# Placing the loads in a slot's DMA queue, and one of two masked copies of q on ScalarE

## The chip, the cores and the metric

The kernel runs on one core of a Trainium2 chip. The metric is the time on the device in microseconds, taken from the slowest core, which here is the only one; lower is better. Before the change three runs gave 944.01 us as their median (943.09 to 948.07).

The engines are named as in the profile: PE multiplies matrices, DVE (VectorE) and POOL (GpSimd) do elementwise work, ACT (ScalarE) applies functions and copies, SP (SyncE) issues nearly all transfers. Each engine works through its own list of instructions in order, and waits at an instruction whose inputs or buffers are not ready.

## The reference

Sixteen sequences of 256 tokens with 256 features go through one cross-attention layer and then one decoder block. All of it is float32, with 16 heads of 16 features.

```
layer 0   q = rmsnorm(x) Wq;  k, v = rmsnorm(ctx) Wk, Wv
          x = rmsnorm(x + attention(q, k, v) Wo)
layer 1   h = layernorm(x);  q, k, v from h, q and k rotated (rope)
          x = x + causal attention(q, k, v) Wo + bias
layer 2   h = layernorm(x);  q from h, k and v from ctx, q and k rotated
          x = x + attention(q, k, v) Wo + bias
MLP       x = x + gelu(layernorm(x) W1 + b1) W2 + b2
```

With 16 sequences there are 48 attentions, and 16 MLPs that are done two sequences at a time.

## The kernel before

**Slots.** The main loop `for i in range(N_ATT)` (L983) has 48 passes, which this text calls slots; slot i does the scores and exponentials of attention i. `ORDER` says which layer each is of: the three layers are interleaved, so that the sequences move through them at different times. The layers of slots 4 to 8 are 1 only in 5 and 7; causal slots followed by one of layer 1 or 2 are slots 21, 28, 38, 40 and 42, and each of those five is followed by layer 2. Batches are loaded for the layer-0 attentions, `xT` and `yT` (turned, 256 KB each), `cur` and `y` (by token, 256 KB each).

**Blocks of a slot.** A slot has four blocks, or three when the attention is causal. Block n writes the scores S of one piece (`scores`, L551), followed on PE by the products of the piece before with v (`values`, L590). ACT turns S into exponentials pt (L562), on causal ones POOL then zeroes what lies above the diagonal (L569). Between blocks PE gets one dense product each: the next attention's q in block 0, its k in block 1, its v in the block before the last, and an older attention's output projection in the last. A causal slot has k and v both in block 1.

**q and k.** A head has 16 features, but a row group of PE has 32 partitions. So two heads share a group and q is kept twice in tile `qm`, once with the odd heads set to zero and once with the even ones: for layers 1 and 2, `q` (L474) multiplies the rotated q by two `parity` columns, on DVE (L487). Rotating (`rotated`) takes ACT's two bias activations (L461), then on DVE a shuffle (L465), two products (L469) and a sum, L485 for q and L510 for k (`kT`). The scores of slot i+1 need both halves of its qm and its kT. For layer 0, nothing is rotated: `q` writes both halves on DVE (L480), and ACT copies kT (L512).

**The way of the sums.** The products with v also give each row's sum of exponentials, as one more column. For an attention, ACT copies the first half of the result out of PSUM (`take`), DVE the second one slot later (`end`, L607), and both halves go to DRAM (`hop`, L608). From there the sums are read back alone (L615), then the rest (`oT`, L620). `invert` takes their reciprocal on DVE (L627), sends it to DRAM (`inv_hop`, L629) and reads it back spread over partitions (`inv`, L635). A slot later `divide` (L641) multiplies. In non-causal slots k follows `invert` in DVE's list, in causal ones it comes ahead of it.

**The SP queue.** Transfers are issued by SP in program order, and SP stands still at one whose input isn't ready. In a slot the order is: the second `hop` of attention i-1, its `sums` and `oT`, the four `hT` of a normalized input that was sent through DRAM (L450) if there is one, then loads (first call of `load_next`, L1015), `inv_hop`, `inv`, `rq` for layer 0, loads again (second call, L1043), the first `hop` of attention i, and `turn_hop` (L441) if an input is sent out. `load_next` (L976) takes its loads from the list `due`: eleven pieces of weights, and ahead of them the four of a batch whose layer-0 attention is three slots ahead. It takes two at a call in a slot with such a batch, otherwise one (none in the first slots).

**Statistics.** A layer-0 attention's `stats` read `cur` and `y` on DVE (L254) two slots before its own.

After the slots follow the MLPs, from about 717 us on.

Of the kernel before, what the change touches and what calls it, by code (L numbers as in the profile page):

```python
# [11 lines left out]
AF = mybir.ActivationFunctionType  # L12
ALU = mybir.AluOpType
# [15 lines left out]
N_ATT = 3 * B  # L29
# [44 lines left out]
def xattn_kernel(  # L74
# [21 lines left out]
    nc = tc.nc  # L96
# [23 lines left out]
    def batch(b):  # L120

        xTs[b] = work.tile([P, KC, S], F32, tag="xT", name=f"xT{b}", bufs=3)
        yTs[b] = work.tile([P, KC, S], F32, tag="yT", name=f"yT{b}", bufs=Y_LIVE)
        ys[b] = work.tile([P, NC, D], F32, tag="y", name=f"y{b}", bufs=3)
        return [
            (rows_of(b), x[b].rearrange("(c p) d -> p c d", p=P)),
            (ys[b], y[b].rearrange("(c p) d -> p c d", p=P)),
            (xTs[b], xt[b].rearrange("(k p) s -> p k s", p=P)),
            (yTs[b], yt[b].rearrange("(k p) s -> p k s", p=P)),
        ]  # L130
# [218 lines left out]
    class Att:  # L349
# [121 lines left out]
                )  # L471
            return a, u

        def q(self):  # L474
            ps = by_feature(self.hT, self.w, 0)
            self.qm = work.tile([P, KC, 2, S], F32, tag="qm", name="qm", bufs=2)
            if self.layer == 0:
                rq = self.rq.unsqueeze(1).to_broadcast([P, KC, S])
                for i in range(2):
                    nc.vector.scalar_tensor_tensor(  # L480
                        self.qm[:, :, i, :], ps, parity[i], rq, ALU.mult, ALU.mult
                    )
                return
            a, u = self.rotated(ps, 0)
            nc.vector.tensor_tensor(a, a, u, ALU.add)  # L485
            for i in range(2):
                nc.vector.tensor_scalar(self.qm[:, :, i, :], a, parity[i], None, ALU.mult)  # L487

        def first_qk(self):

# [171 lines left out]
    def att(i):  # L662
        if i is not None and 0 <= i < N_ATT:
            return atts.setdefault(i, Att(i))
        return None

    def do(i, *names):
        a = att(i)
        for name in names:
            if a is not None:  # L670
                getattr(a, name)()
# [266 lines left out]
    with tc.manual_schedule():  # L938
# [34 lines left out]
            due.append((fc2_sb[:, 2 * j : 2 * j + 2], fc2[j * D : (j + 1) * D]))  # L973
        due = [(t, w.rearrange("(k p) n -> p k n", p=P)) for t, w in due]

        def load_next(i):  # L976
            n = 2 if i > 1 and ahead is not None and ahead.layer == 0 else int(i > 2)
            for t, w in due[:n]:
                nc.sync.dma_start(out=t, in_=w)
            del due[:n]  # L980

        turns = turned_ahead()
        for i in range(N_ATT):  # L983
            a, last = att(i), att(i - 1)
            sent, due_turn = turns.get(i), i + 2 if i + 2 not in turns.values() else None
            fresh = sent is not None and att(sent).below == i - 3
            ahead = att(i + 3)
            if i > 1 and ahead is not None and ahead.layer == 0:
                due[:0] = batch(ahead.b)

            finishing = i >= 3 and att(i - 3).layer == 0
            follows = finishing and i + 2 < N_ATT and att(i + 2).below == i - 3
            for n in range(len(a.blocks)):
                if n == 0 and a.causal and not finishing:
                    do(due_turn, "stats")
                a.scores(n)
                if n > 0:
                    a.values(n - 1)  # L1000
                elif last is not None:
                    last.values(-1)
                final = len(a.blocks) - 1
                if n == 0:
                    if i == 0:
                        a.v()
                        do(1, "spread")
                    late = finishing and i + 2 < N_ATT and att(i + 2).layer == 0
                    if not follows and not late and (finishing or not a.causal):
                        do(due_turn, "stats")  # L1010
                    if sent is not None and not fresh:
                        do(sent, "stats")
                    do(i - 1, "end")
                    do(turns.get(i - 1), "pieces_in")
                    load_next(i)  # L1015
                    if late:
                        do(due_turn, "stats")
                    do(i - 3, "finish")
                    if follows:
                        do(due_turn, "stats")  # L1020
                    if fresh:
                        do(sent, "stats")
                    if not finishing:
                        do(due_turn, "norm")
                    if i == N_ATT - 3:
                        mlps[0].stats()
                    if i == N_ATT - 2:
                        mlps[0].norm()
                    do(i - 2, "divide")
                    if i == N_ATT - 1:  # L1030
                        mlps[0].turn(nc.vector.tensor_copy)
                        mlps[0].keep()
                    do(i + 1, "q")
                elif n == 1:

                    if a.causal:
                        do(i + 1, "k")
                    if last is not None:
                        last.invert(lambda: do(i + 2, "send"))
                    else:  # L1040
                        do(i + 2, "send")
                    do(i + 2, "receive")
                    load_next(i)  # L1043
                    if not a.causal:
                        do(i + 1, "k")
                    if finishing:
                        do(due_turn, "norm")
                    for j in kept.get(i, ()):
                        att(j).keep()
                    if i == N_ATT - 1:  # L1050
                        do(i - 2, "project")
                        mlps[1].norm()
                if n == final - 1:
                    do(i + 1, "v")
                    do(sent, "pieces_out")
                    if i == N_ATT - 2:
                        mlps[1].stats()
                    if i == N_ATT - 1:
                        mlps[0].up(2)
                        mlps[0].mix("hT", HT_LIVE)  # L1060
                if n == final:
                    if i == N_ATT - 1:
                        mlps[1].turn(nc.vector.tensor_copy)
                    else:
                        do(i - 2, "project")
                    do(due_turn, "turn")
                if i == 0 and n == 0:
                    load(4)
                    nc.sync.dma_start(out=bias_sb, in_=rows.partition_broadcast(P))
                    nc.sync.dma_start(out=turn_sb, in_=turn)  # L1070
                if i == 0 and n == 1:
                    load_w(ca_sb, ca[:1], nc.sync)
                if i == 1 and n == 0:
                    load_w(sao_sb, [sa_o], nc.sync)
                if i == 1 and n == 2:
                    nc.sync.dma_start(
                        out=rope_sb, in_=rope.rearrange("(c p) t d -> p c t d", p=P)
                    )
                if i == 1 and n == 3:
                    att_hop = fold_bias(  # L1080
                        [(sa_sb, j * D, V_B1) for j in range(3)] + [(ca_sb, 0, V_B2)]
                    )
                if i == 2 and n == 2:
                    att_cols = fold_back(att_hop)
                    row_v = fc2_sb[:, 0]
                    nc.sync.dma_start(out=row_v, in_=att_hop[2].partition_broadcast(P))
                if i == 2 and n == 3:
                    fold_gain(sa_sb, slice(0, 3 * D), V_G1)
                if i == 3 and n == 3:
                    fold_att(att_cols, row_v)  # L1090
                if i == 8 and n == 2:
                    fold_gain(ca_sb, slice(0, D), V_G2)
                if i == 11 and n == 3:
                    fc1_hop = fold_bias([(fc1_sb, j * D, V_B3) for j in range(4)])
                if i == 12 and n == 1:
                    fc1_cols = fold_back(fc1_hop)
                if i == 14 and n == 2:
                    fold_fc1(fc1_cols)
                if i in (14, 15) and n == 1:
                    fold_gain(fc1_sb, slice(0, FF), V_G3, [i - 14], nc.gpsimd)  # L1100
                if n == 1 and i > 15 and not a.causal:
                    next(combined, None)
# [488 lines left out]
```

## Time and profile before

| | |
|---|---|
| median of three runs (lowest to highest) | 944.01 us (943.09 to 948.07) |
| the profiled execution: its time, its span | 935.7 us, 933.8 us |
| granted PE clock | 0.999 |
| busy PE / DVE / ACT / POOL | 920.2 / 679.2 / 533.2 / 314.0 us |
| second mask and first mask of q, DVE L487 | 64 instructions, 34.1 us |
| DVE idle until sums had landed, L626 and L627 | 15.4 and 13.1 us, 7 and 8 times |
| DVE idle until inv had landed, L641 | 13.0 us, 8 times |
| DVE idle until cur or y had landed, L254 | 1.7 us, 3 times, and 0.2 us, once |
| SP until hop had landed, L615; until inv_hop had landed, L635 | 120.0 us and 76.2 us |
| moved by the DMA engines | 95.26 MB, 102 GB/s over the span |

The span runs from the first to the last instruction of one profiled execution. A group of the profile gives line, engine, operation, output and input, how often, busy time and mean duration in ns, and then the idle time ahead of it with what ended it. In the timeline each line has its start, its duration, engine, source line and operation; "x2" means two instructions in one row. The duration of a DMA row is that of its issue on SP, not of the transfer. Busy time on an engine with idle time costs nothing by itself; what counts is which wait ends last ahead of the engine that sets the time.

### The profile page before, as it was taken

Reading aid. Unit: us, or ns where it says so; the run is one execution under the profiler, and the core shown is the slowest. Engines: PE = TensorE matmul, PEld = TensorE weight load, DVE = VectorE, ACT = ScalarE, POOL = GpSimd, SP = SyncE. Lnnn points to the kernel's source line nnn. Section 1 sums busy time; section 2 is a strip of 40 time slices with the busy share of each in tenths; the row PEclk is TensorE's granted clock in tenths of the full one; section 3 lists DMA queues with packets and bytes.
Section 4 is the critical chain, followed back from the end, with each engine's and each line's share of the span. In section 5 each row is a group of like instructions: output and inputs, shape, how many; then the busy total and the mean of one; then the engine's idle time right before and its main releaser. Section 6 shows DMA issues by size and latency. Waiting matters only on the chain.

```text
span 933.8 us, 29304 instructions
## 1 busy us (share of the span) xinstructions
PE 920.2 (99%) x12266; PEld 540.2 (58%) x12266; DVE 679.2 (73%) x1486; ACT 533.2 (57%) x749; POOL 314.0 (34%) x503
## 2 busy tenths in 40 slices
PE   8999999999999999999999999999999999999997
PEld 4444444445454544454454445455444799999997
DVE  4458677886878787868966878897887566667663
ACT  4666655766666665756656666666666634344440
POOL 4213543324444464443533434344033121122200
PEclk9999999999999999999999999999999999999999
DMA  9434454454334343432435433223222100000001
GB/s 297 155 100 126 128 170 136 132 159 125 124 106 144 94 129 98 152 111 84 141 121 157 132 106 98 90 86 102 92 76 82 36 24 23 20 4 24 24 24 48
DMA packets 115550, 95.26 MB, mean 102 GB/s; under 512 B 23498, under 2 KB 112210, under 8 KB 115410
## 3 DMA queue, kind: packets, MB, share of 16 engines
q1 hardware_dynamic: 114722, 92.77, 31.8%
q8 instruction: 98, 1.61, 0.7%
q10 hardware_dynamic: 688, 0.54, 0.2%
q14 instruction: 42, 0.34, 0.1%
HBM read 57.08 MB, written 36.20 MB: 100 GB/s over the span
## 4 chain that ended last, share of the span: by engine, by line
PE 78%; DVE 11%; DMA 5%; issue 2%; SPq 2%; POOL 2%; ACT 1%; DVEq 0%
PE S L551 15%; PE A L590 14%; PE d L341 13%; PE d L329 13%; PE upX L752 6%; PE A L850 5%; PE downZ L850 3%; PE upZ L752 3%; DVE u L469 2%; PE d L850 2%; DVE a L469 2%; PE d L752 2%; DVE u L465 1%; PE d L286 1%; DMA hop<-av 1%
## 5 line engine op out<-in xcount | busy, mean ns | idle before, releaser
L562 ACT ACTIVATE pt<-S 128x1024 f32<-128x1024 f32 x224 | 217.3, 1022 | 135.3 <-PE S L551 135.0
L551 PE MATMUL S<-qm,kT 32*128 32x512 f32 (+1 forms) x1536 | 202.8, 599 | 4.1 <-DVE kT L510 3.6
L590 PE MATMUL A<-pt,va 128*32 128x256 f32 (+1 forms) x3072 | 191.2, 367 | 1.3 <-POOL pt L569 0.7
L590 PEld LDWEIGHTS A<-pt,va 128*32 128x32 f32 x3072 | 80.5, 109 | 157.0 <-issue 92.7
L562 ACT ACTIVATE pt<-S,sy 128x1024 f32<-128x1024 f32 x128 | 135.7, 1111 | 50.8 <-PE S L551 50.5
L569 POOL TENSOR_SCALAR_AFFINE_SELECT pt<-pt 128x512 f32<-128x512 f32 x128 | 90.7, 725 | 147.5 <-ACT pt L562 146.6
L551 PEld LDWEIGHTS S<-qm,kT 32*128 32x128 f32 x1536 | 62.8, 183 | 76.0 <-issue 41.2
L317 POOL TENSOR_TENSOR cur<-cur,bias 128x512 f32<-128x512 f32 x48 | 68.7, 1438 | 56.5 <-DVE xn L271 56.5
L461 ACT ACTIVATE a<-d,qk_bias 128x256 f32<-128x256 f32 x128 | 53.8, 471 | 52.5 <-PE d L329 31.1
L329 PE MATMUL d<-hT,sa 128*32 128x256 f32 x1024 | 61.1, 379 | 0.0
L246 POOL TENSOR_SCALAR r_ln<-bmv 128x2 f32<-128x2 f32 x48 | 15.3, 318 | 118.0 <-DVE bmv L265 116.5
L469 DVE TENSOR_TENSOR u<-u,turn 128x512 f32<-128x512 f32 x64 | 52.2, 816 | 0.0
L469 DVE TENSOR_TENSOR a<-a,turn 128x512 f32<-128x512 f32 x64 | 49.8, 777 | 2.2
L641 DVE TENSOR_TENSOR oT<-oT,inv 128x512 f32<-128x512 f32 x48 | 39.2, 818 | 14.2 <-DMA inv<-inv_hop 13.0
L607 DVE COPY av<-A 128x512 f32<-128x512 f32 x47 | 32.2, 684 | 22.7 <-PE A L590 22.3
L465 DVE STREAM_SHUFFLE u<-a 128x512 f32<-128x512 f32 x64 | 47.4, 741 | 0.0
L790 ACT ACTIVATE g<-g,fb 128x256 f32<-128x256 f32 x96 | 41.0, 499 | 11.1 <-DVE g L779 11.1
L329 PEld LDWEIGHTS d<-hT,sa 128*32 128x32 f32 x1024 | 33.2, 110 | 22.0 <-issue 0.2
L246 POOL TENSOR_SCALAR r_o<-ms_o 128x2 f32<-128x2 f32 x16 | 3.9, 242 | 122.3 <-DVE sq L254 112.7
L650 DVE TENSOR_TENSOR cur<-d,cur 128x512 f32<-128x512 f32 x32 | 21.6, 676 | 29.0 <-PE d L341 29.0
L271 DVE TENSOR_SCALAR xn<-cur,bmv,r_ln 128x256 f32<-128x256 f32 x96 | 41.5, 481 | 0.8 <-POOL r_ln L247 0.8
L845 DVE TENSOR_TENSOR g<-g,g 128x512 f32<-128x512 f32 x64 | 40.9, 681 | 0.0
(148 smaller groups left out, 1556.0 us busy)
## 6 DMA issues: line engine op xcount, KB each, us to landing
hop<-av SPq DMA_DIRECT2D x96, 256.0 KB
oT<-hop SPq DMA_DIRECT2D x96, 128.0 KB
inv<-inv_hop SPq DMA_DIRECT2D x96, 128.0 KB
turn_hop<-turn SPq DMA_DIRECT2D x23, 256.0 KB
hT<-turn_hop SPq DMA_DIRECT2D x92, 64.0 KB
xT<-in_xt SPq DMA_DIRECT2D x16, 256.0 KB
cur<-in_x SPq DMA_DIRECT2D x16, 256.0 KB
yT<-in_yt SPq DMA_DIRECT2D x16, 256.0 KB
```

What stands on the lines that cost most here:

```text
L317: nc.gpsimd.tensor_tensor(t, t, bias_sb[:, row : row + D].unsqueeze(1).to_broadcast([P, NC, D]), ALU.add)
L329: nc.tensor.matmul(o, lhsT=w[:, k, at + t * P + j : at + t * P + j + 32], rhs=tokens, start=(k == 0), stop=(k == KC - 1), skip_group_check ...
L341: nc.tensor.matmul(ps[j : j + 32, c * D : (c + 1) * D], lhsT=some_tokens(src, k, c, j), rhs=w[:, k, at : at + D], start=(k == 0), stop=(k ...
L461: nc.scalar.activation(a[:, t], ps[:, t], AF.Identity, bias=bias[:, t : t + 1])
L465: nc.vector.stream_shuffle(u.rearrange("p t s -> p (t s)"), a.rearrange("p t s -> p (t s)"), SWAP)
L469: nc.vector.tensor_tensor(t, t, table.unsqueeze(1).to_broadcast([P, KC, S]), ALU.mult)
L551: nc.tensor.matmul(ps[:, j, 2 * m * u : 2 * m * (u + 1)] .rearrange("p (i s) -> p i s", i=2), lhsT=self.kT[r, t, kc * P : (kc + 1) * P], r ...
L562: nc.scalar.activation(pt[:, :, :w], ps[:, :, :w], AF.Exp, scale=scale)
L569: nc.gpsimd.affine_select(out=diag, in_=diag, compare_op=ALU.is_ge, fill=0.0, base=0, pattern=[[0, 2], [0, 2], [1, P]], channel_multiplier=-1,
L590: nc.tensor.matmul(self.av[32 * r : 32 * r + 32, i, q0:S], lhsT=self.va[:, kc, 8 * t + 2 * r + i, :], rhs=pts[r // 2][:, r % 2, i * m : (i ...
L752: nc.tensor.matmul(banks[c // 2][:, (c % 2) * S : (c % 2 + 1) * S], lhsT=a[:, c * P : (c + 1) * P], rhs=b, start=(first and c % 2 == 0), s ...
L850: nc.tensor.matmul(ps[:, c, :], lhsT=a[f // 2][:, f % 2, c * P : (c + 1) * P], rhs=b[:, f, :], start=(first and c == 0 and f == 0), stop=True,
```

## The change

It has two parts.

The loads are called at three places of a slot in place of two. A batch's `cur` and `y` go ahead of the slot's first work, so ahead of the second `hop` of the attention before; `xT` stays behind `inv` and `rq`; `yT` moves from there to the end of the slot, behind the first `hop` and `turn_hop`. Of the weights one is taken at the start of a slot and one behind `inv`, none at the end; in a slot with a batch up to two at the start, one behind `inv` and one at the end are taken from the list, the batch first.

In a causal slot whose next attention is of layer 1 or 2 (the five named above) DVE writes only the first half of qm. The second half is written by ACT from the same rotated q, as a copy with the parity column as its scale. It stands in ACT's list behind k's two bias activations, ahead of the exponentials of the last block. The order of PE's and of POOL's instructions is unchanged.

```diff
-        def q(self):
+        def q(self, both=True):
...
             nc.vector.tensor_tensor(a, a, u, ALU.add)
-            for i in range(2):
-                nc.vector.tensor_scalar(self.qm[:, :, i, :], a, parity[i], None, ALU.mult)
+            nc.vector.tensor_scalar(self.qm[:, :, 0, :], a, parity[0], None, ALU.mult)
+            self.rotated_q = a
+            if both:
+                nc.vector.tensor_scalar(self.qm[:, :, 1, :], a, parity[1], None, ALU.mult)
+
+        def second_mask(self):
+            if self.layer > 0:
+                nc.scalar.activation(
+                    self.qm[:, :, 1, :], self.rotated_q, AF.Copy, scale=parity[1]
+                )
...
-        def load_next(i):
-            n = 2 if i > 1 and ahead is not None and ahead.layer == 0 else int(i > 2)
+        def load_next(i, n, later):
+
+            if not (i > 1 and ahead is not None and ahead.layer == 0):
+                n = later if i > 2 else 0
             for t, w in due[:n]:
                 nc.sync.dma_start(out=t, in_=w)
             del due[:n]
...
             if i > 1 and ahead is not None and ahead.layer == 0:
                 due[:0] = batch(ahead.b)
+            load_next(i, 2, 1)
...
                     do(turns.get(i - 1), "pieces_in")
-                    load_next(i)
...
-                    do(i + 1, "q")
+                    if i + 1 < N_ATT:
+                        att(i + 1).q(both=not a.causal)
                 elif n == 1:
                     if a.causal:
-                        do(i + 1, "k")
+                        do(i + 1, "k", "second_mask")
...
                     do(i + 2, "receive")
-                    load_next(i)
+                    load_next(i, 1, 1)
...
                     do(due_turn, "turn")
+                    load_next(i, 1, 0)
```

## The prediction

> **What bounds the kernel now.** I read the page's busy times first, then its groups, then who PE waited for, and last the timeline around those waits.
>
> ```profile
> span 933.8 us, 29304 instructions
> ...
> PE 920.2 (99%) x12266; PEld 540.2 (58%) x12266; DVE 679.2 (73%) x1486; ACT 533.2 (57%) x749; POOL 314.0 (34%) x503
> ...
> L551 PE MATMUL S<-qm,kT 32*128 32x512 f32 (+1 forms) x1536 | 202.8, 599 | 4.1 <-DVE kT L510 3.6
> ```
>
> PE is busy 920.2 of 933.8 us at a granted clock of 0.999, and the change adds or removes no matmul. So at most the 13.6 us of PE's idle time can be won. The largest named part of it is 3.6 us of scores waiting for kT; the rest lies at the start, in hundredths between matmuls, or in the MLP tail, which the change does not touch. The timeline of PE shows the eight waits singly (the last bracket is the idle time and its releaser):
>
> ```profile
> 119.16 1.14 PE L551 MATMUL S<-qm,kT 32*128 32x512 f32 x8 [0.94 <-DVE kT L510]
> 339.69 1.14 PE L551 MATMUL S<-qm,kT 32*128 32x512 f32 x8 [0.37 <-DVE kT L510]
> 355.98 1.14 PE L551 MATMUL S<-qm,kT 32*128 32x512 f32 x8 [0.59 <-DVE kT L510]
> 442.04 1.14 PE L551 MATMUL S<-qm,kT 32*128 32x512 f32 x8 [0.37 <-DVE kT L510]
> 587.55 1.14 PE L551 MATMUL S<-qm,kT 32*128 32x512 f32 x8 [0.36 <-DVE kT L510]
> 616.31 1.14 PE L551 MATMUL S<-qm,kT 32*128 32x512 f32 x8 [0.36 <-DVE kT L510]
> 645.67 1.14 PE L551 MATMUL S<-qm,kT 32*128 32x512 f32 x8 [0.37 <-DVE kT L510]
> 662.21 1.14 PE L551 MATMUL S<-qm,kT 32*128 32x512 f32 x8 [0.25 <-DVE kT L510]
> ```
>
> Five of them, 0.36 to 0.37 each, open slots 22, 29, 39, 41 and 43. Each of these follows a causal slot whose successor is not of layer 0, and ORDER has exactly five such pairs: the ones the new mask is for. Slot 21's timeline shows why kT is late:
>
> ```profile
> 334.30 0.84 ACT L461 ACTIVATE a<-d,qk_bias 128x256 f32<-128x256 f32 x2 [0.76 <-PE d L329]
> 335.02 1.51 DVE L487 TENSOR_SCALAR qm<-a,vec 128x512 f32<-128x512 f32 x2
> 336.46 0.72 DVE L465 STREAM_SHUFFLE u<-a 128x512 f32<-128x512 f32 x1
> 337.12 1.94 ACT L562 ACTIVATE pt<-S 128x1024 f32<-128x1024 f32 x2 [1.98 <-PE S L551]
> 338.54 1.00 DVE L510 TENSOR_TENSOR kT<-a,u 128x512 f32<-128x512 f32 x1
> ```
>
> k's biased input is ready at 335.14, but DVE is at the masks until 336.46 and only then begins k's four instructions. ACT meanwhile idles 1.98 us before the next exponentials.
>
> The 0.94 us wait is of the other kind, and the SP queue in slots 5 and 6 carries it:
>
> ```profile
> 101.06 0.43 SPq L979 DMA_DIRECT2D cur<-in_x  x1
> 101.54 0.47 SPq L979 DMA_DIRECT2D y<-in_y  x1
> 102.11 0.41 SPq L629 DMA_DIRECT2D inv_hop<-sums  x1
> 106.09 1.23 SPq L635 DMA_DIRECT2D inv<-inv_hop  x2
> 107.37 1.07 SPq L979 DMA_DIRECT2D xT<-in_xt  x1
> 108.48 0.47 SPq L979 DMA_DIRECT2D yT<-in_yt  x1
> 109.05 0.93 SPq L608 DMA_DIRECT2D hop<-av  x2
> 113.74 0.55 SPq L615 DMA_DIRECT2D sums<-hop  x1
> ```
>
> The 16 KB inv_hop, behind 512 KB of cur and y, lets inv issue only 4.0 us after it. SP stands at that wait, so both hops leave at 109.05, though DVE had copied the second av by 105.95. The sums then arrive at 115.8, and DVE begins k only after their reciprocal.
>
> **What the Trainium skill says.** "SBUF — State Buffer", Who interferes with whom: DVE and GpSimd share one port pair; a tensor_scalar can take it exclusively, a two-input DVE instruction contends for its read side, ACT has ports of its own. The trace agrees: the pair of masks takes 1.51 us beside GpSimd's affine selects and 0.88 where GpSimd is quiet. "ScalarE: Activation LUTs", What ACT_TABLE_LOAD costs: 186 ns + 0.833 ns per element, 93 ns more per pointer operand; its section on table sets has copy in every set, so no reload. The trace has 0.59 us for a 512-wide copy and 1111 against 1022 ns for exponentials with and without a pointer scale: it agrees on the 0.09. "DMA: Bandwidth & Descriptors", Queues, rings and completion order: each DMA engine consumes a ring's descriptors in order. So a load can't be waited round; inv_hop's 4.0 us here against 1.5 (340.50 to 342.01 in slot 21, no load just ahead) agrees.
>
> **The change, part by part.**
>
> *The second mask, five times.* DVE loses the second half of 1.51 us. The first mask took 0.74 in slot 21 and the shuffle began 0.70 after it ended, so 0.70 goes. At the least it is 0.49, the median mask, at the most about 1.0 if the later kT sum also escapes GpSimd. I take 0.70. The PE wait is only 0.37, so it goes wholly: 0.37+0.37+0.36+0.36+0.37 = 1.83 us. Even 0.49 is enough.
>
> ACT gains five activations of 0.59+0.09 = 0.68 us (0.71 by the skill's formula, an estimate). Each stands behind k's two bias activations, ending at 335.14, and waits for DVE's sum a+u, done at 334.98, so it doesn't wait. It ends at about 335.9; the exponentials behind it start at 337.12. The cover is the 1.98 us idle. Without it, each would push the exponentials, the selects and the first half's av copy by up to 0.68, or 3.4 us in all. The qm it writes is needed at 339.3, 3.4 us later.
>
> Behind DVE's k stands the reciprocal, so inv_hop, inv and the next slot's divide come 0.70 earlier too. Slots 22 and 43, whose divides idled 0.69 and 2.25 us for inv, get kT 0.70 earlier while PE is 0.37 earlier: 0.59 becomes 0.26 and 0.25 becomes 0, another 0.33+0.25 = 0.58. Sum of the masks: 2.4 us.
>
> *cur and y ahead of the second hop (11 batches) instead of behind oT and hT.* No work is added. Their two issues (0.90 us) leave the way of inv_hop and enter that of the hop. Where SP stood waiting for av anyway (slot 5: turn_hop issued by 91.01, hop at 92.80) the issue is free; where it didn't (slot 7: turn_hop until 123.09, hop at 123.20) it costs 0.9. The transfer: rq, a weight, two hops and turn_hop, 1.15 MB, issued 121.19 to 123.20, had the hop landed by 127.59, some 180 GB/s; 0.5 MB more costs the hop up to 2.9 us, and nothing where queues were empty. The same transfer in front of inv_hop cost 2.5 (4.0 against 1.5). hop, sums, inv_hop, inv is one chain, so this is near a trade.
>
> In slot 6, inv leaves 0 to 1.5 us earlier, but a weight now goes ahead of its hop (1.3 us): the 0.94 lies between 0 and 1.8, taken as unchanged. In slot 8 the sums come 0 to 3 us later against a kT slack of 0.87 us; I charge 0.6. Slot 32 (slack 0.44) may lose 0.8 or win as much, since its statistics waited 0.90 for cur: 0. In slots 11, 14, 17, 24 and 29 the reciprocal was not waiting for the sums and kT has 1 to 3.7 us: 0.
>
> *yT at a slot's end, weights at its start.* SP reaches yT straight after the first hop, still ahead of the second wherever both left together (slots 6, 8, 22, 32); yT is used a slot and more later. Weights number eleven as before. I take 0, with ±0.5.
>
> **Sum.** -2.4 + 0.6 = -1.8 us. DVE's statistics also waited 1.9 us for cur and y (1.7 and 0.2), which now come half a slot sooner; that a third of it, 0.6, reaches PE is a choice. Together -2.4 on the profiled 935.7 us (span 933.8 and 1.9 around it): 933.3. The median of the runs is 944.0, 8.3 above that execution; nothing shows where these 8.3 lie, so I carry the difference over: **941.6 us**, 0.25% faster. A difference below 0.5%, 4.7 us, can hardly be told from no change here, so "within 0.5%" is 939.3 to 948.7.
>
> **Rivals.**
> 1. *The loads win too.* All eight waits go (-3.6) and part of the 8.3 us by which the timed runs exceed the profile is the same kind of wait on DMA, of which a third goes (-2.8): about 937.6. For it: the spread of the timed runs, 943.1 to 948.1, with a PE that has nothing to vary. Against: the profile has no such waits left beyond the eight.
> 2. *Slower: the hop becomes the late one.* From the point where the load costs the hop more than the slack of kT, PE stands still by the excess. At 2.9 us a pair plus 0.9 of SP: slot 6 +1.8, slot 8 +2.9, slot 32 +2.5, and weights ahead of hops in slots 4 and 10 about +1.2; also slot 30 or 34 with +1: 9.4 - 2.4 = +7.0, 951. For it: causal slots had DVE idle 2 to 3.7 us for the sums already. Against: before its next av copy DVE also idles 2.0 to 2.4 us for PE, which absorbs most of the delay.
> 3. *The mask buys nothing.* ACT's write or GpSimd's port becomes the late one, or the loads give back the 2.4: 944. Against: 3.4 us of room for qm, and 0.70 against 0.37.
>
> **Chances.** Forecast 0.57 (own range 939.8 to 943.5), rival 1 0.16, rival 2 0.11, rival 3 0.16. Faster by over 0.5%: rival 1 and a tail of the forecast less rival 1's weak end, 0.16. Slower by over 0.5%: most of rival 2 and scatter, 0.10. Within: 0.74. Range: 936.5 reaches into rival 1, 947 takes in rival 3 and the weak end of rival 2.
>
> **What would show it.** Right: no kT wait at the openings of slots 22, 29, 39, 41 and 43; five new ACT rows of about 0.68 us just behind k's bias; exponentials behind them unmoved; DVE masks 59 instead of 64; the reciprocals of the causal slots later in 5, 7, 31 and 33, inv_hop to inv near 1.5 us. Wrong: new waits S<-kT in slots 8, 32 or 6 of over 1 us each, a wait of A on av's copy, or PE busy time itself changing.

## The result and the profile after

Side by side, 22 runs each, the changed kernel took 937.96 us (median; 934.07 to 942.17) and the kernel before 942.42 us (937.54 to 949.88): a ratio of 0.9948, interval 0.9928 to 0.9967. So it is faster by 0.5%, with an interval from 0.3 to 0.7%. A second comparison later (22 and 43 runs) gave 937.46 against 942.46, 0.9945 [0.9929, 0.9962]. The forecast was 941.6, a ratio of 0.9975 to the 944.01 that it started from: the right direction, half the size.

The one profiled execution of the changed kernel is no typical one. It took 940.52 us, longer than most of its runs, while the profiled execution of before, 935.7, was shorter than any of the 22 runs beside it. The two profiles by themselves would say that the change costs 5 us. The page of the changed kernel, its first lines, two groups of PE and one of DVE:

```profile
span 938.8 us, 29297 instructions
...
PE 921.5 (98%) x12266; PEld 540.7 (58%) x12266; DVE 677.0 (72%) x1481; ACT 536.5 (57%) x754; POOL 315.2 (34%) x503
...
L559 PE MATMUL S<-qm,kT 32*128 32x512 f32 (+1 forms) x1536 | 203.4, 602 | 5.8 <-DVE kT L518 5.3
L598 PE MATMUL A<-pt,va 128*32 128x256 f32 (+1 forms) x3072 | 192.3, 368 | 2.8 <-DVE av L615 1.1
...
L635 DVE RECIPROCAL sums<-sums 128x32 f32<-128x32 f32 x48 | 16.8, 350 | 32.6 <-DMA sums<-hop 24.7
```

ACT has five instructions more and DVE five fewer, as the diff says. PE's wait for kT is 5.3 us here, not less than the 3.6 of before, and the reciprocal's wait for the sums went from 13.1 to 24.7 us. The timeline of PE says which of the eight waits are left:

```profile
120.26 1.14 PE L559 MATMUL S<-qm,kT 32*128 32x512 f32 x8 [1.69 <-DVE kT L518]
386.40 1.14 PE L559 MATMUL S<-qm,kT 32*128 32x512 f32 x8 [0.25 <-DVE kT L518]
475.76 1.14 PE L559 MATMUL S<-qm,kT 32*128 32x512 f32 x8 [0.46 <-DVE kT L518]
535.44 2.09 PE L559 MATMUL S<-qm,kT 32*128 32x512 f32 x8 [2.95 <-DVE kT L518]
```

These open slots 7, 25, 31 and 35. The five of the mask, slots 22, 29, 39, 41 and 43, are gone, and so are those behind them at slots 23 and 44. What is left is of the other kind, and the chain that ended last shows it in slots 33 and 34 (start, duration, piece; only the sums' way and the loads are kept, and the short "issue" pieces between them are left out):

```profile
507.34 0.45 SPq L989
507.83 0.99 SPq L989
508.87 5.07 DMA hop<-av
...
514.08 2.06 DMA sums<-hop
...
517.89 2.89 DMA inv_hop<-sums
...
523.08 0.47 SPq L989
523.64 6.16 DMA hop<-av
...
529.93 2.15 DMA sums<-hop
...
534.61 0.70 DVE kT L518
...
535.44 2.09 PE S L559 x8
```

`cur` and `y` (L989 at 507) leave just ahead of a second hop, which then takes 5.07 us; `yT` (523.08) stands ahead of the next one, 6.16 us. In slot 33 of the kernel before, no load was issued just ahead of that hop, and SP came from it to its sums in 2.69 us, not 5.21:

```profile
504.92 0.37 SPq L608 DMA_DIRECT2D hop<-av  x1
507.61 0.55 SPq L615 DMA_DIRECT2D sums<-hop  x1
```

Two passes of the sums' way in a row come late, and PE stands 2.95 us. The matmuls behind that stop take 2.09 us in place of 1.14; more on that below. On SP, hops were waited for 137.0 us (before 120.0) and inv_hop 62.2 us (76.2). So 17 us of waiting came to one link of the chain and 14 left another.

### The profile page after: what moved, and what is told of

It reads as the page before. It is cut to its first block, busy times and chain, and to the rows that moved or that the text cites. A ratio compares the mean times of both kernels' runs of the same rounds, so it can differ in the third digit from the quotient of the medians.

```text
span 938.8 us, 29297 instructions
## 1 busy us (share of the span) xinstructions
PE 921.5 (98%) x12266; PEld 540.7 (58%) x12266; DVE 677.0 (72%) x1481; ACT 536.5 (57%) x754; POOL 315.2 (34%) x503
## 4 chain that ended last, share of the span: by engine, by line
PE 76%; DVE 10%; DMA 7%; SPq 2%; issue 2%; POOL 2%; ACT 0%; ACTq 0%; DVEq 0%; POOLq 0%
PE S L559 14%; PE A L598 14%; PE d L341 13%; PE d L329 12%; PE upX L760 6%; PE A L858 5%; DMA hop<-av 4%; PE downZ L858 3%; PE upZ L760 3%; PE d L858 2%; PE d L760 1%; DMA inv_hop<-sums 1%; PE d L286 1%; DMA sums<-hop 1%; DVE u L469 1%
## 5 line engine op out<-in xcount | busy, mean ns | idle before, releaser
L317 POOL TENSOR_TENSOR cur<-cur,bias 128x512 f32<-128x512 f32 x48 | 71.8, 1501 | 56.5 <-DVE xn L271 56.5
L649 DVE TENSOR_TENSOR oT<-oT,inv 128x512 f32<-128x512 f32 x48 | 37.7, 785 | 11.4 <-DMA inv<-inv_hop 7.6
L635 DVE RECIPROCAL sums<-sums 128x32 f32<-128x32 f32 x48 | 16.8, 350 | 32.6 <-DMA sums<-hop 24.7
```

Of the source, the lines that this page charges most:

```text
L317: nc.gpsimd.tensor_tensor(t, t, bias_sb[:, row : row + D].unsqueeze(1).to_broadcast([P, NC, D]), ALU.add)
```

## The experiments

The ratios are to runs of the kernel before in the same session: 59 runs (median 941.4) for the first four experiments, 58 (940.33) for the next four, 43 (942.46) for the last four.

**Only the mask.** The kernel before, with the second mask on ACT in the five slots and the loads where they were (`q` and `second_mask` are those of the change).

```diff
-                    do(i + 1, "q")
+                    if i + 1 < N_ATT:
+                        att(i + 1).q(both=not a.causal)
-                        do(i + 1, "k")
+                        do(i + 1, "k", "second_mask")
```

> The kernel before with the second mask on ACT in the five causal slots, loads as before. Theory A (the masks are the gain, the loads a trade): the kT waits of 0.37 us at the openings of slots 22, 29, 39, 41 and 43 are gone, those slots' predecessors take 12.70 us in place of 13.13, five ACT rows of 0.68 us; time 1.8 to 2.6 us below before, ratio 0.9973 to 0.998. Theory B (the loads carry most of the measured 4.5 us): the same five waits are gone, but the time falls by no more than 1.8 us.

Measured: 937.68 (22 runs), 0.9963 [0.994, 0.9985]; span 933.6. That is some 3.5 us, more than the 1.8 to 2.6 expected, and most of what the whole change gave (0.9948); the intervals overlap. Slot 21 in its timeline, DVE and ACT, to be held against the lines of slot 21 in the prediction:

```profile
336.56 0.84 ACT L461 ACTIVATE a<-d,qk_bias 128x256 f32<-128x256 f32 x2 [0.76 <-PE d L329]
337.27 0.74 DVE L486 TENSOR_SCALAR qm<-a,vec 128x512 f32<-128x512 f32 x1
337.33 0.73 ACT L493 ACTIVATE qm<-a,vec 128x512 f32<-128x512 f32 x1
337.94 0.72 DVE L465 STREAM_SHUFFLE u<-a 128x512 f32<-128x512 f32 x1
339.32 1.94 ACT L570 ACTIVATE pt<-S 128x1024 f32<-128x1024 f32 x2 [1.26 <-PE S L559]
340.03 0.69 DVE L518 TENSOR_TENSOR kT<-a,u 128x512 f32<-128x512 f32 x1
```

From the start of the masks to the end of kT it is 340.72 - 337.27 = 3.45 us, where it was 339.54 - 335.02 = 4.52 with both masks on DVE. That is 1.07 us, and 1.07 to 1.10 in all five slots. Of it 0.77 is the mask: the shuffle begins 0.67 us behind the start of the masks, where it was 1.44. The rest is the last sum, 0.69 in place of 1.00. It now begins 0.39 us ahead of POOL's next selects, where before it began 0.32 us behind them; that POOL is what had slowed it fits this, but was not tried by itself. ACT's write took 0.72 us, and its idle time ahead of the exponentials went from 1.98 to 1.26: they didn't move.

**Only the loads.** The three places of the changed kernel (with its `load_next`), both masks on DVE.

```diff
                 due[:0] = batch(ahead.b)
+            load_next(i, 2, 1)
...
                     do(turns.get(i - 1), "pieces_in")
-                    load_next(i)
...
                     do(i + 2, "receive")
-                    load_next(i)
+                    load_next(i, 1, 1)
...
                     do(due_turn, "turn")
+                    load_next(i, 1, 0)
```

> The new places of the loads alone, both masks on DVE. Theory A: the five waits of 0.37 us stay, inv_hop is waited for less and hop and sums more, and the time lies within 2 us of before, ratio 0.998 to 1.002. Theory B: 2 to 4 us below before, ratio 0.9957 to 0.998, with slots 6 and 22 shorter than in before.

Measured: 942.69 (14 runs), 1.0005 [0.998, 1.003]. The loads by themselves are worth nothing that can be seen. Who PE waited for, and below it who DVE waited for (us in total, times, longest):

```profile
PE S L559 <- DVE kT L518: 4.5, 8, 1.7
```

```profile
DVE sums L634 <- DMA sums<-hop: 26.8, 10, 4.6
DVE sums L635 <- DMA sums<-hop: 25.3, 14, 5.6
```

The five waits of 0.35 to 0.36 us at the mask's slots are all there again. The one at slot 7 is 1.69 as in the changed kernel. It was 1.28 to 1.69 us in the four traces with `cur` and `y` early, and 0.41 to 1.17 in the four with all loads in their old places (the kernel before, the mask alone, and two more below). So it may go with the loads, but three traces with `yT` alone moved have 0.70, 0.76 and 1.98: single executions scatter as far. The changed kernel's wait of 2.95 us at slot 35 is not there. DVE's waits for the sums, 52.1 us in all, were 28.5 before. The wait for inv (L649) fell from 13.0 to 5.2 us in exchange.

**cur and y early, yT where it was.** As above, but `yT` stays with `xT` behind inv.

```diff
                     do(i + 2, "receive")
-                    load_next(i, 1, 1)
+                    load_next(i, 2, 1)
...
                     do(due_turn, "turn")
-                    load_next(i, 1, 0)
```

> As e2, but yT stays with xT behind inv; cur and y and the weights go to the slot's start. Both masks on DVE. If the pair's place is what moves the time, this equals e2 within 1 us. DVE's wait for cur and y (1.9 us) goes, its waits for sums in causal slots 5, 7, 31 and 33 grow by 1 to 3 us each.

Measured: 939.92 (14 runs), 0.9988 [0.9962, 1.0015]. Not told apart from no change, nor from the loads alone, which it was expected to equal.

**yT late, cur and y where they were.** The other half of the move alone.

```diff
                     do(turns.get(i - 1), "pieces_in")
-                    load_next(i)
+                    load_next(i, 2, 1)
...
                     do(i + 2, "receive")
-                    load_next(i)
+                    load_next(i, 1, 1)
...
                     do(due_turn, "turn")
+                    load_next(i, 1, 0)
```

> As before, but yT goes to the slot's end, behind the first hop and turn_hop; cur, y and the weights stay behind oT and hT. Both masks on DVE. Theory A: no change, within 1 us of before, since SP reaches yT before the second hop all the same. Theory B's variant that yT is what stood in the sums' way: 1.5 us or more below before, and slots 6, 8, 22 and 32 shorter.

Measured: 939.6 (22 runs), 0.9977 [0.9955, 0.9998]: a gain of 0.2% whose interval just leaves out zero. Among twelve comparisons one such edge is weak evidence; what it is worth beside the mask is looked at twice below.

**No batch loads at all.** The four loads of eleven batches are left out; GpSimd sets their tiles to 0.5 instead, so the kernel computes with constants in their place.

```diff
-                nc.sync.dma_start(out=t, in_=w)
+                if w is None:
+                    nc.gpsimd.memset(t, 0.5)
+                else:
+                    nc.sync.dma_start(out=t, in_=w)
...
-                due[:0] = batch(ahead.b)
+                due[:0] = [(t, None) for t, _ in batch(ahead.b)]
```

> The kernel before, both masks on DVE, but the four loads of each of the 11 batches taken in the slots are left out and GpSimd fills the tiles with 0.5 instead (the output is not the reference's). It bounds what any placing of these loads could win. If the loads trade one delay of the sums' chain for another (theory A), taking them out wins all of it: kT waits other than the five of 0.37 us gone, 1.5 to 4 us below before, and the runs scatter less. If they cost next to nothing where they are, it lies within 1.5 us of before.

Measured: 934.79 (8 runs, 933.31 to 935.92), 0.9934 [0.9909, 0.9959]. All of these loads together cost about 5.5 us of 940 (3.9 to 8.6 by the interval), which is about as much as placing them can win. And most of the scatter goes with them: 2.6 us from end to end in 8 runs, where the 58 runs of the kernel before beside it lay 10.8 us apart. Of PE's waits for kT in the trace, only the one at slot 7 went. Those at slots 23 and 44 (0.57 and 0.26 us) stayed, against what was expected, and slots 30 and 31 waited 0.20 and 1.08. The two profiled spans differ by 1.2 us only (933.8 and 932.6), so most of the loads' cost lies in executions that are slower than the one profiled before.

**The mask on ACT in every slot.** In the non-causal slots behind the third block's exponentials.

```diff
-                        att(i + 1).q(both=not a.causal)
+                        att(i + 1).q(both=False)
...
+                if n == 2 and not a.causal:
+                    do(i + 1, "second_mask")
```

> As e1, and in the 27 other slots ahead of a layer-1 or layer-2 attention the second mask goes to ACT too, behind the third block's exponentials; loads as before. DVE loses 27 more masks of 0.48 us ahead of the reciprocal and k, ACT gains 27 of 0.72. If kT is late through DVE's work in non-causal slots as well, the kT waits at slots 7, 9, 23 and 44 shrink by up to 0.5 us each and the time falls 1 to 2 us below e1. If the sums set them, or ACT becomes late, it lies within 1 us of e1 or above.

Measured: 937.73 (22 runs), 0.9964 [0.994, 0.9987], the same as with five. So no worth of the other 27 masks was seen; with intervals of some 2 us either way, a small one could hide. In those slots k stands behind the reciprocal and so behind the sums, which would explain it, but was only argued.

**The mask and yT late.** The first and the fourth experiment together.

> e1 and e4 together: the second mask of the five slots on ACT, yT at the slot's end, cur and y and weights behind oT and hT as before. If both effects add, 3.6 + 1.8 = 5 us below before, and below after by 1. If e4 was scatter, it equals e1.

Measured: 935.17 (20 runs), 0.9937 [0.9917, 0.9957], the lowest median of a kernel that makes all its loads. It was run again beside the changed kernel (last experiment).

**The mask without its cover.** ACT writes the second half five times over.

```diff
-                nc.scalar.activation(
-                    self.qm[:, :, 1, :], self.rotated_q, AF.Copy, scale=parity[1]
-                )
+                for _ in range(5):
+                    nc.scalar.activation(
+                        self.qm[:, :, 1, :], self.rotated_q, AF.Copy, scale=parity[1]
+                    )
```

> As e1, but ACT writes each of the five second halves five times over (same values). ACT's 1.98 us of idle time ahead of the exponentials covers one write of 0.72 us, with 1.26 to spare. Five take 3.6 us, so the exponentials of the last block start about 1.6 us later, the selects and the first half's av copy with them. If the cover is what makes the mask free, PE now waits in the next slot's first block, by 0.5 to 1.5 us in each of the five, and the time is 2.5 to 7 us above e1. If ACT's lateness doesn't matter there, it equals e1.

Measured: 944.84 (22 runs), 1.0044 [1.0024, 1.0064], 7.2 us above the mask written once, which ran in the session before. Its timeline, ACT in slot 21 and PE at the openings of the five slots:

```profile
343.26 3.74 ACT L494 ACTIVATE qm<-a,vec 128x512 f32<-128x512 f32 x5
346.90 1.92 ACT L571 ACTIVATE pt<-S 128x1024 f32<-128x1024 f32 x2
...
347.96 2.04 PE L560 MATMUL S<-qm,kT 32*128 32x512 f32 x8 [0.45 <-ACT pt L571]
450.33 2.04 PE L560 MATMUL S<-qm,kT 32*128 32x512 f32 x8 [0.45 <-ACT pt L571]
596.63 2.04 PE L560 MATMUL S<-qm,kT 32*128 32x512 f32 x8 [0.46 <-ACT pt L571]
626.38 2.04 PE L560 MATMUL S<-qm,kT 32*128 32x512 f32 x8 [0.44 <-ACT pt L571]
656.71 2.04 PE L560 MATMUL S<-qm,kT 32*128 32x512 f32 x8 [0.45 <-ACT pt L571]
```

The exponentials now follow the writes without a pause. The four further writes take 3.74 - 0.73 = 3.01 us, the cover left was 1.26, so they overhang by 1.75. Of that PE loses 0.45 at the first tile and 2.04 - 1.14 = 0.90 inside the row, where the second tile waits too (the granted clock stayed at 1.00 there): 1.35 a slot, 6.75 us in five, against the 7.2 measured. The cover was real, and this is what its end costs.

**The mask without the batch loads.** The first and the fifth experiment together, with the same loads left out.

> The kernel before with the second mask on ACT in the five slots, and with the four loads of eleven batches left out (GpSimd sets those tiles to 0.5, so the output is not the reference's). Without these loads the runs of the kernel before lay within 933.3 to 935.9, so the mask can be read here without their scatter. Theory that the masks save PE's waits: DVE 1.08 us earlier in five slots against waits of 0.36 each, with the knock-on in the slots behind, 1.8 to 2.4 us: 934.8 becomes 932.4 to 933.0. Rival, that part of what the masks won (3.5 us with loads) was a changed meeting with the loads: less than 1.5 us here, 933.3 or more. If the masks are worth 3.5 us of themselves: 931.3.

Measured: 930.32 (6 runs, 930.13 to 930.75), 0.9879 [0.9853, 0.9904]. Held against the 934.79 without the mask, 4.5 us; the two are of different sessions. That is more than each of the three sizes expected. With the scatter gone, the openings of the slots in the two traces can be subtracted one by one (time without the mask less time with it, and its growth):

```
slot opened      22    23    24    29    30    31    39    41    43    44
difference     0.80  1.44  1.61  2.03  2.31  2.70  3.13  3.57  4.01  4.33
growth         0.43  0.64  0.17  0.43  0.28  0.39  0.43  0.44  0.44  0.32
```

Up to slot 21 the difference stands at 0.37, from the start of the program, and between the steps it doesn't move by more than 0.02. Five direct steps make 2.17 us, the five behind them 0.64 + 0.17 + 0.28 + 0.39 + 0.32 = 1.80: 3.97 us for the mask. The page's groups show PE's waits for kT, the last figure, without the mask and with it:

```profile
L551 PE MATMUL S<-qm,kT 32*128 32x512 f32 (+1 forms) x1536 | 202.4, 599 | 4.3 <-DVE kT L510 3.9
```

```profile
L559 PE MATMUL S<-qm,kT 32*128 32x512 f32 (+1 forms) x1536 | 202.4, 600 | 1.1 <-DVE kT L518 0.7
```

They are 3.2 of the 3.97 us. Most of the rest is 0.07 us at each opening that lost its wait: in the timeline, rows that follow without a stop overlap by 0.07 us (one of 1.14 us is followed after 1.07), and a stop loses this besides its own length. The step at slot 24 is a wait of 0.23 us for POOL in the slot before, which is gone.

**All four loads late.** The mask, `cur` and `y` behind inv, `xT` and `yT` at the slot's end: no batch load is issued between the start of a slot and its `inv`.

```diff
                     do(turns.get(i - 1), "pieces_in")
-                    load_next(i)
+                    load_next(i, 0, 1)
...
                     do(i + 2, "receive")
-                    load_next(i)
+                    load_next(i, 2, 1)
...
                     do(due_turn, "turn")
+                    load_next(i, 2, 0)
```

> Masks on ACT; no batch load ahead of a second hop or of inv_hop: cur and y behind inv, xT and yT at the slot's end, each pair behind the short transfers of its half slot. Theory that a load is costly where the short transfers of the same half slot queue behind it: inv_hop to inv near 1.5 us and the second hop to sums as in the kernel before, 934 to 936. Rival, that any place costs the same, since the rings pass the same bytes in a slot and the 0.5 MB at a slot's end meets the next slot's second hop: 937 to 939, as with the masks alone.

Measured: 953.43 (6 runs), 1.0124 [1.0094, 1.0155], slower than either kernel; both expectations missed. From inv_hop to inv SP now took 1.90 us in the mean of the eleven slots with a batch, where it was 2.75 in the kernel before (2.31 in the changed one). But the loads have a date of their own. Who PE waited for, and then who DVE waited for:

```profile
PE A L598 <- DVE av L615: 13.9, 5, 4.7
```

```profile
DVE sq L254 <- DMA cur<-in_x: 25.3, 7, 6.4
```

and the chain in slot 22:

```profile
348.87 4.73 DMA cur<-in_x
...
355.46 0.61 DVE av L615
...
356.12 1.92 PE A L598 x13
```

DVE's list has the statistics of `cur` ahead of the copy of av. `cur` lands at 353.60, the statistics and then the copy follow, and PE stands 4.7 us for it. The clock adds to it: the granted clock fell to 0.50 behind two of these stops, 4.7 and 4.2 us, and was 0.990 in the mean of the execution, against 0.999 with the mask alone.

**The changed kernel and the mask with yT late, once more.** In one session.

> The changed kernel itself again, beside the two that follow on the same chip. Theory that its loads are a trade: 937 to 939, a ratio to the kernel before of 0.993 to 0.998. Rival, that the loads help a little of themselves: 935 to 936.

> Masks on ACT, cur and y with xT's old places, yT alone at the slot's end, as in the earlier run at 935.2. Theory that yT's move is worth 1 to 3 us and moving cur and y ahead of the second hop costs that again: 934.5 to 936.5, 1 to 3 us below the changed kernel beside it. Rival, that the earlier difference was scatter: within 1 us of the changed kernel.

Measured: 937.46 (22 runs), 0.9945 [0.9929, 0.9962], and 936.5 (22 runs), 0.9944 [0.9925, 0.9963]. The advantage seen before isn't confirmed: no version was shown to be better than the changed kernel. The estimates for the mask with its loads in three different places (0.9963; 0.9948 and 0.9945; 0.9937 and 0.9944) lie within 0.3% of each other, and their intervals overlap: what the loads do beside the mask stays open at that size.

## Why the prediction was half right

**The five waits** (predicted 1.83 us): right in kind and place. They are gone, and each gives 0.43 to 0.44, not 0.36 to 0.37, because of the 0.07 us of overlap: 2.17 us.

**DVE's saving** (0.70 taken, "about 1.0 if the later kT sum also escapes GpSimd"): this is the term that was mis-sized, and with it the mask's worth. The upper bound was the true value, 1.07 us in slot 21: 0.77 for the mask and 0.30 for the sum.

**The knock-on** (0.58): its rule was right and its input wrong. The rule was DVE's gain less PE's: with 0.70 - 0.37 it gave 0.33 for slot 22's end; with 1.07 - 0.43 it gives 0.64, which is what slot 23 opened earlier. Measured 1.80 in all, at five openings, where the prediction followed only the two that the profile showed as waits, slots 23 and 44. Openings 24, 30 and 31 gained too: without loads, kT waits of 0.20 and 1.08 us at 30 and 31 became 0 and 0.68. Mask in sum: 2.4 predicted, 3.97 without loads; with them about 3.5 (0.9963 of 941.4, interval 1.4 to 5.6).

**ACT's write** (0.68 on a cover of 1.98): 0.72, the cover left 1.26, exponentials unmoved; uncovered it costs PE 1.35 a slot for an overhang of 1.75.

**The loads** (+0.6 and -0.6): right as a sum, 1.0005 [0.998, 1.003], but wrong in its places, so that the sum came out owes something to luck: the -0.6 was called a choice when it was made. Slot 6 was given 0 to 1.8 us and taken as unchanged; the wait at its end grew from 0.94 to 1.69, which is no more than such traces scatter. Slot 8, charged 0.6, and slot 32 showed no new wait. The late one was slot 34, at whose end PE waited 2.95 us (3.09 in the second trace of the changed kernel), which stood in the second rival as one of two doubtful slots at 1 us. The trace of the loads alone has the same loads there and no such wait, so it isn't the loads' place by itself that makes it; what else does is open. That rival's mechanism is what happens, a hop late by more than kT's slack; it doesn't happen often enough to turn the sign.

**The signs.** DVE wrote 59 masks, ACT had five new rows of 0.72 us, and the reciprocals waited longer for the sums, as forecast. inv_hop to inv came down from 2.75 to 2.31 us in the mean of the slots with a batch, not to near 1.5. And two signs of being wrong came, though small: A waited 1.13 us for av's copy in slot 25, and PE's busy time went from 920.2 to 921.5 us (924.8 in the second trace), with the granted clock at 0.998 and 0.996 in place of 0.999. The forecast had not reckoned with that, and the first rival took PE as having nothing to vary.

**The first rival** (the loads win too, 937.6) came nearer in time than the forecast and is still refuted in kind: the loads alone won nothing that can be seen.

**The 8.3 us between the profile and the runs**, carried over as unexplained: 1.6 of them are the small number of runs, since the median of before, 944.0 in three, is 942.4 in 22. Most of the other 6.7 goes with the batch loads: without them the median falls by 5.5 us, and the runs lie at 933.3 to 935.9, a range that holds the profiled 935.7. So the execution profiled before was one that the loads hardly hurt. Of the 3.6 us by which the forecast time was missed, 1.6 is that median; the other 2.0 is in the effect, 4.5 us measured against 2.4, and 1.6 of it the mask's 3.97 for 2.4.

## What to carry to other kernels

An operation taken off an engine can be worth more than its own time, as here where the sum behind it also got shorter; follow that gain to the next wait behind, not only to the first. A load moved off one link of a chain of small transfers lands on another link, or past its own date, so put a price on both ends of its window before you move it. When runs scatter by more than the effect, leave out what makes the scatter: without the loads an effect of 4 us could be read slot by slot.

## What was not expected of the hardware

**A stop of PE can cost more than itself.** The second profile of the changed kernel has PE waiting 2.01 us in slot 12, and then:

```profile
204.31 2.99 PE L559 MATMUL S<-qm,kT 32*128 32x512 f32 x8 [2.01 <-ACT pt L570]
207.23 1.94 PE L598 MATMUL A<-pt,va 128*32 128x256 f32 x16
208.94 3.07 PE L341 MATMUL d<-sa,hT 128*32 128x256 f32 x32
211.94 1.14 PE L559 MATMUL S<-qm,kT 32*128 32x512 f32 x8
213.01 1.07 PE L598 MATMUL A<-pt,va 128*32 128x256 f32 x16
```

The first three rows take 8.00 us where 1.14 + 1.07 + 1.91 = 4.12 is usual. The table of stretches gives the granted clock (the third figure from the end, behind POOL's):

```profile
204.00:206.00 2.00, 1.69 (x6) 0.90 (x8) 1.93 (x4) 1.90 (x4) 0.00 (x0) 0.62 0.04 12
206.00:208.00 2.00, 2.00 (x14) 0.40 (x12) 1.70 (x7) 1.68 (x2) 0.00 (x0) 0.50 0.16 41
208.00:210.00 2.00, 2.00 (x24) 0.98 (x20) 1.93 (x4) 0.96 (x2) 0.00 (x0) 0.50 0.69 213
210.00:212.00 2.00, 2.00 (x31) 0.78 (x20) 0.49 (x1) 0.00 (x0) 0.00 (x0) 0.68 0.12 25
212.00:214.00 2.00, 2.00 (x30) 0.90 (x32) 1.88 (x5) 0.83 (x1) 0.00 (x0) 1.00 0.41 137
```

So a wait of 2.0 us cost another 3.9. The clock's part, from the shares of the table, is 2 x (0.38 + 0.50 + 0.50 + 0.32) = 3.4 us; the other 0.5 is in the first row, whose second tile waits for its own exponentials, as above where the mask lost its cover. In the first profile the stop of 2.95 us was followed by rows of 2.09 and 1.52 us, another 1.4.

The Trainium skill, "TensorE: Matmul & The Clock Gate", Part 1, What's actually happening, tells of the two clocks, half and full, and of an idle window of about 3.4 us that runs free of the program. The halves agree. The length doesn't quite: the clock fell to 0.50 behind stops of 1.16 (the loads alone, slot 12), 1.89, 2.01, 2.08 and 2.95 us, while stops of 1.69, 1.98, 3.09 and 3.31 us left the next rows at their usual 1.14 and 1.07 us. So between 1.16 and 3.31 us the length alone doesn't decide. The stops of 1.16, 1.89 and 2.01 us also had that second pause in the row behind them. Where in the window a stop falls may be the rest of it; that wasn't tried.

This can turn a small delay of a load into a larger one, and so into scatter. Of 160 runs of the kernel before, the 88 with a mean granted clock of 0.999 or more averaged 940.1 us, the 31 below 0.997 averaged 945.8. It shows what goes together, not which came first.

**A load can hold SP.** A load of weights ahead of slot 6's hop kept SP at its issue for 2.73 us, where 41 of the 55 rows of such issues took 0.43 to 0.49:

```profile
108.11 2.73 SPq L989
110.94 3.85 DMA hop<-av
```

What held it the profile doesn't name.
